# A selective scan whose initial values are folded into the first decay of each chunk

## The chip, the cores and the metric

The kernel runs on one core of one Trainium2 chip. The metric is device time in microseconds (us), from launch to end, as the median of several runs. A core has five engines with instruction streams of their own: PE (TensorE, matrix products), DVE (VectorE), ACT (ScalarE, activation functions), POOL (GpSimd) and SP (SyncE, which here issues transfers). [...] SBUF and PSUM are the two on-chip memories, both with 128 partitions.

## The reference

Two layers of a vision state-space model run one after the other on an image batch of 8 x 64 x 64 x 192. Each layer normalizes, projects to 384 channels, runs a 3x3 depthwise convolution, and scans the 4096 pixels of every image in several directions (layer 0: two, layer 1: four). Cut to the part that matters, the scan of one direction is:

```python
def step(h, inp):                                  # h: [b, K, 384, 16]
    u_t, dl_t, B_t, C_t = inp
    dA = jnp.exp(dl_t[..., None] * As[None])       # the decay
    h = dA * h + (dl_t * u_t)[..., None] * B_t[:, :, None, :]
    y = jnp.einsum('bkdn,bkn->bkd', h, C_t)
    return (h, y)
_, ys = lax.scan(step, h0, (u_l, dl_l, B_l, C_l))  # h0 = 0
```

`dl_t` is a softplus of a projection of the input. Each of 384 channels has 16 states, so there are 6144 independent first-order recurrences for each image and direction. Afterwards the directions are added, layer-normalized, gated and projected back.

## The kernel before, in words

**Tiling.** The 384 channels are three groups of 128 partitions (`DT = 3`). The 4096 pixels are cut into eight chunks of `T = 512`, the 16 states into eight pairs (`NP = 8`). One chunk of one direction of one image is a step `i`. It has 24 slots (`NSL`): a slot is one pair of states `m` and one channel group `dt`. There are 128 steps in layer 0 and 256 in layer 1; the eight steps of one direction of one image, a pass, follow one another, and `ci` counts them from 0. Half of the directions run backwards through the pixels (`rev`).

**What a slot does.** On PE, `inject` (L693) makes the inputs `hb` of the two recurrences in PSUM (two buffers). On ACT, `decay` (L713) makes the two rows of decays `da`, two Exps over 512 elements with the channel's `a_neg` as scale (five buffers). On DVE, `scan` (L728) runs two `tensor_tensor_scan` instructions: each computes o[t] = a[t] * o[t-1] + v[t] along 512 elements and needs a value to start from. In the first chunk of a pass that is the constant 0.0; in the other seven it is a column of the small tile `st`, which holds the states at the end of the chunk before. On POOL the result `h` is multiplied with the broadcast `C` rows (`cr`) into `hc`. On PE `reduce` (L752) sums `hc` over states into `py`. Every third slot `carry` (L747), on ACT, copies the last column of `h` (the first in a backward pass) into `st`. `h` has two buffers and `hc` and `cr` three, each for three slots.

**What else is in a step.** While step i is scanned, the inputs of step i+1 are prepared: `dt_proj` and `dt_bias` (the projection, L613 and L625), `dt_softplus` (L637, a softplus over `delta` with an ACT table load in front of it and one behind it that brings back the exponential set), `turn_delta` and `make_dut` (L655, L663). Finishing work of the image before (functions `f_...`: normalization, gate, output projection) is spread over the steps: in layer 0 in a rhythm of two steps, in layer 1 of four. Most of PE's small results go through one PSUM bank, tag "m", which holds one tile at a time.

**What sets the order.** Nothing is scheduled automatically here. `at(i, s, f, ...)` notes that function f is issued at slot s of step i; slot numbers stand in the tables `L0_SLOTS` and `L1_SLOTS`. At each slot the loop at L1049 issues the scan, then what is noted for the slot, then `inject` for two slots ahead and `decay` for four slots ahead. Each engine takes its instructions in this order, and waits are added where data or buffers demand it.

Of the kernel before, what the change touches and what calls it, by code (L numbers as in the profile page):

```python
# [8 lines left out]
F32 = mybir.dt.float32  # L9
AF = mybir.ActivationFunctionType  # L10
# [5 lines left out]
P = 128  # L16
# [8 lines left out]
DT = 3  # L25
NS = 16
T = 512
# [6 lines left out]
NP = NS // 2  # L34
# [476 lines left out]
def scans(tc, name, x_src, x_dst, xcd, xcd_col, xtd, xdd, t, dirs, rank, row_b, gate, slots, last, consts, dram):  # L511
# [5 lines left out]
    nc = tc.nc  # L517
# [3 lines left out]
    dtb, a_neg, lnw, lnb = t["dtb"], t["a_neg"], t["lnw"], t["lnb"]  # L521
    K = len(dirs)
    R = row_b + 2 * NS
    NSL = NP * DT
# [13 lines left out]
    steps = []  # L538
# [6 lines left out]
    with tc.tile_pool(name=f"{name}_s1", bufs=1) as s1, tc.tile_pool(  # L545
        name=f"{name}_s2", bufs=2
    ) as s2, tc.tile_pool(name=f"{name}_psy", bufs=1, space=PSUM) as psy, tc.tile_pool(
        name=f"{name}_psh", bufs=2, space=PSUM
    ) as psh:
        st = s1.tile([P, DT, 2, NP], F32, name="st")  # L550
        todo = {}

        def at(i, s, f, *a):
            todo.setdefault(i * NSL + s, []).append((f, a))

        live = {}
# [80 lines left out]
        def dt_softplus(i):  # L637
            softplus(nc, live[i]["delta"], live[i]["delta"])

            nc.scalar.preload_act_table_set("natural_log_exp_and_others")  # L640

        def load_xt(i):

            b, k, cols, rev, ci, c = steps[i]
            live[i]["xt"] = s1.tile([P, GC, D], F32, name="xt_k")
            for r in range(2):
                if cols:
                    w = c * RB + r * GC
                    src = xtd[b].rearrange("(h w) d -> h w d", w=W)[:, w : w + GC]
                else:  # L650
                    l = c * T + r * GC * G
                    src = xtd[b][l : l + GC * G].rearrange("(g j) d -> j g d", j=G)
                nc.sync.dma_start(out=live[i]["xt"][r * G : (r + 1) * G], in_=src)
# [59 lines left out]
        def decay(g):  # L713

            i, s = divmod(g, NSL)
            m, dt = divmod(s, DT)
            k = steps[i][1]
            da = s2.tile([P, 2, T], F32, name="da", bufs=5)
            for n in range(2):
                nc.scalar.activation(  # L720
                    da[:, n].rearrange("p (r g j) -> p r g j", r=2, j=G),
                    live[i]["delta"][:, dt].rearrange("p (g r j) -> p r g j", r=2, j=G),
                    AF.Exp,
                    scale=a_neg[:, k, dt, 2 * m + n : 2 * m + n + 1],
                )
            live[i]["da", s] = da

        def scan(i, s):  # L728
            m, dt = divmod(s, DT)
            b, k, cols, rev, ci, c = steps[i]  # L730
            hb, da = live[i].pop(("hb", s)), live[i].pop(("da", s))
            if dt == 0:
                live[i]["h", m] = (
                    s2.tile([P, DT, 2, T], F32, name="h"),
                    s2.tile([P, DT, 2, T], F32, name="hc", bufs=3),
                )
            h, hc = live[i]["h", m]
            for n in range(2):
                o, a = h[:, dt, n], da[:, n]
                v = hb.rearrange("p r (j n) -> p n (r j)", n=2)[:, n]  # L740
                if rev:
                    o, a, v = o[:, ::-1], a[:, ::-1], v[:, ::-1]
                init = 0.0 if ci == 0 else st[:, dt, n, m : m + 1]
                nc.vector.tensor_tensor_scan(o, a, v, init, ALU.mult, ALU.add)  # L744
            nc.gpsimd.tensor_mul(hc[:, dt], h[:, dt], live[i]["cr", m])  # L745

# [193 lines left out]
        def thrice(i, s, f, *a):  # L940
            for p, q in enumerate(s):
                at(i, q, f, *a, p)

        for i in range(N):
            j = i - 1
            live[i] = {}
            at(j, -3, load_xt, i)
            if xdd is None:
                at(j, -8, load_x, i)
                thrice(j, slots["x_proj"], x_proj, i)  # L950
                at(j, slots["x_dbl"], x_dbl, i)
            else:
                at(j, -4, load_xdbl, i)
            at(j, slots["turn_b"], turn_b, i)
            at(j, slots["keep_b"], keep_b, i)
            for dt in range(DT):
                for f in dt_proj, dt_bias, turn_delta, make_dut:
                    at(j, slots[f.__name__][dt], f, i, dt)
            at(j, slots["softplus"], dt_softplus, i)
            at(i, -12, load_b, i, 0)  # L960
            at(i, 0, load_b, i, 1)
            for m in range(NP):
                at(i, 3 * m - 6, load_c, i, m)
                at(i, 3 * m + 3, carry, i, m)
                for n in range(2):
                    at(i, 3 * m + slots["reduce"][n], reduce, i, m, n)
            b, k, cols, rev, ci, c = steps[i]
            if k and dirs[k - 1][0] != cols:
                for j in range(4 * DT):
                    at(i, 8 + j, load_turned, i, j)  # L970
                at(i, slots["add_turned"], add_y, i)
            else:
                at(i, 6, load_y, i)
                at(i, slots["add_y"], add_y, i)
            at(i, slots["keep_y"], keep_y, i)
# [24 lines left out]
        for c in range(NCH):  # L1000
            b, e, own = B - 1, N - NCH + c + 1, last
# [45 lines left out]
        with tc.manual_schedule(engines=ENGINES):  # L1047
            g = min(todo)
            while todo:  # L1049
                i, s = divmod(g, NSL)  # L1050
                if 0 <= g < N * NSL:
                    scan(i, s)
                for f, a in sorted(todo.pop(g, []), key=lambda fa: rank_of.get(fa[0], 1.5)):
                    f(*a)
                if 0 <= g + 2 < N * NSL:
                    inject(g + 2)
                if 0 <= g + 4 < N * NSL:
                    decay(g + 4)
                g += 1


def vss_layer(tc, name, x_src, x_dst, w, dirs, rank, row_b, gate, slots, last, consts, dram):

    with ExitStack() as ctx:
        xcd, xcd_col, xtd, xdd, *dram = dram
        if any(cols for cols, rev in dirs):
            xdd = None
        else:
            xcd_col = None
        t = load_weights(tc, ctx, name, w, len(dirs), rank, row_b + 2 * NS, consts[1])  # L1070
        clear = dram[-1] if xcd_col is None else ()
        front(tc, name, x_src, xcd, xcd_col, xtd, xdd, w["in_proj"][:, :D], t, clear, consts)
        scans(tc, name, x_src, x_dst, xcd, xcd_col, xtd, xdd, t, dirs, rank, row_b, gate, slots, last, consts, dram)
# [99 lines left out]
```

## Time and profile before

| What | us |
|---|---|
| Median of three runs | 25840.9 (25839.86 to 25843.88) |
| The profiled execution's own time | 25837.38 |
| Its span, first to last instruction | 25835.2 |
| of it before the scans of layer 0 (normalization, projection, convolution) | 954.8 |
| scans of layer 0, 128 steps | 8064.2, 63.0 each |
| before the scans of layer 1 | 1128.9 |
| scans of layer 1, 256 steps | 15650.8, 61.1 each |
| the end after the last scan | 36.5 |

The stretches are read from the starts and ends of scan instructions in the timeline. In layer 0's scan stretch DVE is busy for 7737.5 us and PE for 7553.0; in layer 1's DVE for 15184.5 us, PE for 14786.6, POOL for 14642.7 and ACT for 10885.3. The mean granted clock of TensorE was 0.991. DMA moved 160 GB/s on average.

In the groups of the page a line gives the source line, the engine, the operation, the tiles written and read with their shapes, and how often it ran; then the busy time in us with the mean duration of one in ns; then the idle time of its engine just ahead of it and who ended most of that. Where instructions of one engine overlap, the busy time counts a moment once, so it can be less than the count times the mean.

### The profile page before, as it was taken

The page shows a single profiled execution, that of the slowest core. Times are in us where ns is not written, and L with a number is a line of the kernel's source. Part 1 is how long each engine was busy: PE and PEld are TensorE (multiplying, and loading weights), DVE is VectorE, ACT ScalarE, POOL GpSimd, SP SyncE. Part 2 cuts the span into 40 slices and gives each one's busy share as a digit, 9 for nine tenths or more (in the row PEclk, how much of TensorE's full clock was granted, in tenths as well). Part 3 has the DMA queues.
Part 4 walks back from the last instruction along what each step waited for, and adds up shares of the span by engine and source line. Part 5 has one row for each costly group of instructions (what it writes and reads, how often), then busy time and mean ns, then how long its engine had stood idle before and what let it go on. Part 6 is the DMA issues. An engine that isn't in the chain of part 4 may idle for free.

```text
span 25835.2 us, 786127 instructions
## 1 busy us (share of the span) xinstructions
PE 24166.5 (94%) x340032; PEld 13568.7 (53%) x340032; DVE 24275.9 (94%) x22142; ACT 17771.4 (69%) x28068; POOL 22094.0 (86%) x9615
## 2 busy tenths in 40 slices
PE   9999999999999988999999999999999999999999
PEld 4555555555555534555555555555555555555554
DVE  7899999999999856999999999999999999999998
ACT  5667777777777656667666766766767767766766
POOL 0499999999999702999999999999999999999997
PEclk9999999999999999999999999999999999999999
DMA  4566666666666545575575575575575575575574
GB/s 164 153 154 156 154 156 158 155 155 156 154 157 156 133 161 173 164 160 165 166 161 167 166 160 166 166 161 167 166 161 167 166 159 167 165 161 167 164 163 141
DMA packets 3836347, 4140.60 MB, mean 160 GB/s; under 512 B 2140460, under 2 KB 2340804, under 8 KB 3829828
## 3 DMA queue, kind: packets, MB, share of 16 engines
q1 hardware_dynamic: 3821296, 4032.72, 60.5%
q8 instruction: 2692, 44.11, 0.7%
q10 hardware_dynamic: 11604, 57.59, 0.6%
q14 instruction: 755, 6.18, 0.1%
HBM read 3443.63 MB, written 645.99 MB: 158 GB/s over the span
## 4 chain that ended last, share of the span: by engine, by line
DVE 25%; PE 24%; issue 6%; ACT 6%; DMA 0%; POOL 0%; DVEq 0%; SPq 0%; ACTq 0%; POOLq 0%
DVE h L744 23%; PE hb L703 11%; PE py L151 7%; PE pd L568 2%; PE pt L616 2%; ACT da L720 2%; DVE dut L666 1%; PE pz L843 1%; ACT delta L144 1%; PE po L922 1%; ACT L144 1%; ACT L640 1%; ACT delta L630 1%; PE pq L658 0%; ACT xn_sq L831 0%
## 5 line engine op out<-in xcount | busy, mean ns | idle before, releaser
L745 POOL TENSOR_TENSOR hc<-h,cr 128x1024 f32<-128x1024 f32 x9216 | 21629.2, 2368 | 3610.2 <-DMA xt_k<-xtd 2022.4
L744 DVE TENSOR_TENSOR_SCAN h<-da,st,hb 128x512 f32<-128x512 f32 x16128 | 19191.2, 1259 | 625.2 <-PE hb L703 541.2
L720 ACT ACTIVATE da<-delta,a_neg 128x512 f32<-128x512 f32 x18432 | 12142.9, 713 | 3210.4 <-DVE h L744 3204.1
L703 PEld LDWEIGHTS hb<-dg,dut 64*128 64x128 f32 x147456 | 9256.7, 185 | 7063.8 <-issue 5863.5
L703 PE MATMUL hb<-dg,dut 64*128 64x128 f32 x147456 | 10905.4, 286 | 896.3 <-DVE h L744 622.7
L151 PE MATMUL py<-hc,mask 32*32 32x512 f32 x147456 | 6871.1, 602 | 0.2
L151 PEld LDWEIGHTS py<-hc,mask 32*32 32x32 f32 x147456 | 1568.4, 103 | 2341.7 <-issue 1746.8
L744 DVE TENSOR_TENSOR_SCAN h<-da,hb 128x512 f32<-128x512 f32 x2304 | 2611.3, 1200 | 121.7 <-PE hb L703 113.7
L750 ACT COPY st<-h 128x6 f32<-128x6 f32 x2688 | 533.0, 198 | 1843.4 <-DVE h L744 1842.3
L616 PE MATMUL pt<-xdbl,w_dt 96*128 96x512 f32 (+1 forms) x2304 | 1301.1, 646 | 53.3 <-DVE yc L886 33.4
L355 DVE SCALAR_TENSOR_TENSOR tp<-pad,cw,tp 128x512 f32<-128x512 f32 x1344 | 988.3, 750 | 214.6 <-ACT tp L349 180.5
L658 PE MATMUL pq<-ident,delta 128*128 128x128 f32 x4608 | 760.4, 288 | 388.7 <-DVE dut L666 334.6
L630 ACT ACTIVATE delta<-pt,dtb 128x512 f32<-128x512 f32 x1152 | 783.8, 680 | 477.4 <-PE pt L616 477.0
L843 PE MATMUL pz<-xn_sq,w_in 96*128 96x512 f32 x1536 | 832.0, 641 | 36.3 <-ACT xn_sq L831 15.8
L666 DVE TENSOR_TENSOR dut<-pq,xt_k 128x512 f32<-128x512 f32 x1152 | 767.1, 666 | 81.0 <-PE pq L658 81.0
L568 PE MATMUL pd<-x_k,w_x 128*128 128x512 f32 x1536 | 798.1, 629 | 38.8 <-DVE yc L886 15.2
L922 PE MATMUL po<-yc,w_out 128*96 128x512 f32 x1536 | 782.8, 620 | 15.4 <-POOL yc L916 12.4
L658 PEld LDWEIGHTS pq<-ident,delta 128*128 128x128 f32 x4608 | 485.1, 141 | 588.0 <-DVE dut L666 473.4
L151 PE MATMUL pc<-pad,taps 32*32 32x512 f32 x13824 | 578.0, 593 | 19.1 <-ACT xo L370 17.0
L916 POOL TENSOR_TENSOR yc<-yc,g 128x512 f32<-128x512 f32 x384 | 490.1, 1279 | 109.3 <-ACT yc L907 106.4
L144 ACT ACTIVATE delta<-delta 128x1536 f32<-128x1536 f32 x384 | 570.5, 1486 | 4.3
L322 PE MATMUL pi<-x,w_x 128*128 128x512 f32 x768 | 407.2, 650 | 165.9 <-ACT x L302 116.5
(103 smaller groups left out, 9927.5 us busy)
## 6 DMA issues: line engine op xcount, KB each, us to landing
cr<-cscr SPq DMA_DIRECT2D x2048, 512.0 KB
dg<-dgd SPq DMA_DIRECT2D x1536, 512.0 KB
cr<-xdd SPq DMA_DIRECT2D x1024, 512.0 KB
xt_k<-xtd SPq DMA_DIRECT2D x768, 384.0 KB
xcd<-xo SPq DMA_DIRECT2D x128, 768.0 KB
xtd<-xv SPq DMA_DIRECT2D x128, 768.0 KB
y<-yrow SPq DMA_DIRECT2D x128, 768.0 KB
yc<-yrow SPq DMA_DIRECT2D x128, 768.0 KB
```

The source lines that it names most:

```text
L144: nc.scalar.activation(out, in_, AF.Softplus)
L151: nc.tensor.matmul(out[j * Q : (j + 1) * Q, dt], w[i * Q : (i + 1) * Q], x[i * Q : (i + 1) * Q], start=first, stop=last, tile_position=(i ...
L568: nc.tensor.matmul(live[i]["pd"][:R], w_x[:, dt, k, :], live[i]["x"][:, dt], start=(dt == 0), stop=(dt == DT - 1),)
L616: nc.tensor.matmul(pt, w_dt[:, k, dt * P : (dt + 1) * P], live[i]["xdbl"][:rank], start=True, stop=True,)
L630: nc.scalar.activation(live[i]["delta"][:, dt].rearrange("p (g r j) -> p r g j", r=2, j=G), live[i]["pt"].rearrange("p (r g j) -> p r g j" ...
L658: nc.tensor.transpose(pq[:, g], live[i]["delta"][:, dt, g * P : (g + 1) * P], ident)
L703: nc.tensor.matmul(hv[:, r, q], live[i]["dut"][r * G : (r + 1) * G, dt, q], dg[r * G : (r + 1) * G, q, :, 2 * mm : 2 * mm + 2], start=True ...
L720: nc.scalar.activation(da[:, n].rearrange("p (r g j) -> p r g j", r=2, j=G), live[i]["delta"][:, dt].rearrange("p (g r j) -> p r g j", r=2 ...
L744: nc.vector.tensor_tensor_scan(o, a, v, init, ALU.mult, ALU.add)
L745: nc.gpsimd.tensor_mul(hc[:, dt], h[:, dt], live[i]["cr", m])
L843: nc.tensor.matmul(fin["pz"], w_in[:, u, dt * P : (dt + 1) * P], fin["xn"][:, u], start=(u == 0), stop=(u == CT - 1),)
L922: nc.tensor.matmul(fin["po"][:CP], w_out[:, dt, u * CP : (u + 1) * CP], fin["y"][:, dt], start=(dt == 0), stop=(dt == DT - 1),)
```

## The change

All scans start from a constant, 1.0 in the chunks that used to start from `st`. What they started from is multiplied into the first decay beforehand: a[0] * s + v[0] is the same as (a[0] * s) * 1.0 + v[0]. "First" is the first column in a forward pass and the last in a backward one (`edge`).

Three pieces make that product. `first_decays`, one slot after the softplus of the coming step, computes the decays of that one column for all 16 states on ACT, into a small tile `a0` of 128 x 3 x 16. `enter`, on POOL, multiplies `a0` by `st`, in two halves: states of the first four pairs at slot 14 of the step before, the other four at slot 1 of the step itself (`NSL + 1` counted from the step before). Last, `decay` copies two elements of `a0` over the edge column of each `da` tile, on ACT behind its two Exps. None of this is issued for the first chunk of a pass. `carry` stays as it was.

```diff
+        def edge(rev):
+            return T - 1 if rev else 0
+
+        def first_decays(i):
+            b, k, cols, rev, ci, c = steps[i]
+            if ci == 0:
+                return
+            live[i]["a0"] = s2.tile([P, DT, NS], F32, name="a0")
+            for dt in range(DT):
+                nc.scalar.activation(
+                    live[i]["a0"][:, dt],
+                    a_neg[:, k, dt],
+                    AF.Exp,
+                    scale=live[i]["delta"][:, dt, edge(rev) : edge(rev) + 1],
+                )
+
+        def enter(i, half):
+            if steps[i][4] == 0:
+                return
+            ms = slice(half * NP // 2, (half + 1) * NP // 2)
+            a0 = live[i]["a0"].rearrange("p t (m n) -> p t m n", n=2)[:, :, ms]
+            nc.gpsimd.tensor_mul(a0, a0, st.rearrange("p t n m -> p t m n")[:, :, ms])
...
@@ decay
                     scale=a_neg[:, k, dt, 2 * m + n : 2 * m + n + 1],
                 )
+            if steps[i][4] > 0:
+                f = edge(steps[i][3])
+                nc.scalar.copy(da[:, :, f], live[i]["a0"][:, dt, 2 * m : 2 * m + 2])
             live[i]["da", s] = da
@@ scan
-                init = 0.0 if ci == 0 else st[:, dt, n, m : m + 1]
+                init = 0.0 if ci == 0 else 1.0
                 nc.vector.tensor_tensor_scan(o, a, v, init, ALU.mult, ALU.add)
@@ the plan, for each step i with j = i - 1
             at(j, slots["softplus"], dt_softplus, i)
+            at(j, slots["softplus"] + 1, first_decays, i)
+            at(j, 14, enter, i, 0)
+            at(j, NSL + 1, enter, i, 1)
```

## The prediction

> **What bounds the kernel now.** I read the page's busy line first, then its costliest groups, then the waits, then busy times chunk by chunk. The busy line:
>
> ```profile
> PE 24166.5 (94%) x340032; PEld 13568.7 (53%) x340032; DVE 24275.9 (94%) x22142; ACT 17771.4 (69%) x28068; POOL 22094.0 (86%) x9615
> ```
>
> No engine is alone at the top; ACT (ScalarE) has most room. The groups concerned:
>
> ```profile
> L745 POOL TENSOR_TENSOR hc<-h,cr 128x1024 f32<-128x1024 f32 x9216 | 21629.2, 2368 | 3610.2 <-DMA xt_k<-xtd 2022.4
> L744 DVE TENSOR_TENSOR_SCAN h<-da,st,hb 128x512 f32<-128x512 f32 x16128 | 19191.2, 1259 | 625.2 <-PE hb L703 541.2
> L720 ACT ACTIVATE da<-delta,a_neg 128x512 f32<-128x512 f32 x18432 | 12142.9, 713 | 3210.4 <-DVE h L744 3204.1
> ...
> L744 DVE TENSOR_TENSOR_SCAN h<-da,hb 128x512 f32<-128x512 f32 x2304 | 2611.3, 1200 | 121.7 <-PE hb L703 113.7
> L750 ACT COPY st<-h 128x6 f32<-128x6 f32 x2688 | 533.0, 198 | 1843.4 <-DVE h L744 1842.3
> ```
>
> The reader is to see two kinds of scan: 16,128 that read their initial value from `st`, and 2,304 (first chunks of a direction) that start from a constant. The second kind is 59 ns shorter. Back to back the instructions overlap, so what counts is the pitch. Four of each in a row, from the timeline:
>
> ```profile
> 987.66 4.54 DVE L744 TENSOR_TENSOR_SCAN h<-da,hb 128x512 f32<-128x512 f32 x4
> ```
> ```profile
> 5023.72 4.79 DVE L744 TENSOR_TENSOR_SCAN h<-da,st,hb 128x512 f32<-128x512 f32 x4
> ```
>
> (4.79 - 4.54)/4 = 62 ns; the median over all start-to-start times is 1171 against 1111 ns, so 60 ns. The waits:
>
> ```profile
> ACT da L720 <- DVE h L744: 3204.1, 3349, 3.2
> DVE h L744 <- PE hb L703: 654.9, 1069, 6.3
> PE hb L703 <- DVE h L744: 622.7, 1142, 1.8
> DVE h L744 <- ACT da L720: 42.2, 52, 2.8
> ```
>
> ACT waits for DVE, seldom the reverse; DVE and PE wait for each other in equal amounts. Last, five consecutive chunks (48 scans each) of layer 1, the first with constant initial values; columns are the stretch, its length, and each engine's busy time:
>
> ```profile
> core 0: us, PE busy (x) PEld busy (x) DVE busy (x) ACT busy (x) POOL busy (x), PEclk, DMA share, GB/s
> 15955.20:16016.30 61.10, 59.81 (x848) 32.82 (x838) 58.58 (x56) 42.48 (x70) 59.70 (x28) 1.00 0.52 152
> 16016.30:16077.40 61.10, 58.83 (x832) 32.27 (x828) 58.80 (x53) 42.34 (x69) 56.37 (x25) 1.00 0.65 189
> 16077.40:16136.40 59.00, 55.51 (x840) 31.34 (x828) 58.41 (x53) 40.60 (x66) 56.37 (x25) 1.00 0.58 160
> 16136.40:16196.50 60.10, 55.87 (x828) 31.59 (x828) 59.97 (x53) 44.29 (x69) 56.20 (x25) 1.00 0.57 163
> 16196.50:16259.40 62.90, 60.23 (x850) 33.01 (x840) 61.39 (x55) 43.61 (x72) 60.36 (x29) 1.00 0.51 148
> ```
>
> Chunks 0 and 4 carry the same finishing work and differ in the scans. This is the change's effect already in the trace: DVE works 2.81 us less in chunk 0, and the chunk is 1.8 us shorter, not 2.8, because PE (98% busy) and POOL (98%) are then in the way. Chunks 2 and 3 are DVE's alone (99% and 99.8%).
>
> **What the Trainium skill says.** "Perfetto Trace Analysis", Optimizing Scalar/DVE Operations, gives a data-access overhead of about 60 ns for DVE on SBUF per instruction. It does not say that a per-partition initial value pays it a second time; the trace shows 60 ns for it. "ScalarE: Activation LUTs", What ACT_TABLE_LOAD costs: an ACTIVATE takes 186 ns + 0.833 ns per element, 93 ns more for a pointer operand, and back-to-back ones overlap by 93 ns. That makes 706 ns for the decays (713 here) and 188 for a two-element copy (the six-element one here: 198). "SBUF — State Buffer", Terms, has DVE and GpSimd exclude each other on a shared port pair. A scan takes one stream from PSUM, and hc products run beside scans all through the timeline, so I charge nothing.
>
> **Part 1, scans from 1.0.** 16,128 x 60 ns = 968 us less on DVE, 2.9 us in each of 336 chunks (seven in eight of 384). I take 1.0 to cost what 0.0 costs, both being constants in the instruction.
>
> **Part 2, a copy behind each pair of decays.** 336 x 24 = 8,064 copies on ACT. In the order of instructions each copy waits for the Exp just before it, so it cannot overlap it: 93 ns of overlap lost, a wait of about 32 ns (the gap between the two dependent Ln and Exp of `pm`, L893 and L894), and 188 ns less the 93 that the next instruction overlaps. Sum 0.22 us per slot, 5.3 us per chunk. The lower bound is 0.11 us, the step from an `st` copy to the next Exp (1004.54 to 1004.65); the upper is 0.35, nothing overlapping and a second such wait (93 + 32 + 198 + 32 ns). ACT then has 46 to 53 us of work in chunks of 58 to 63. Cover: `da` has five buffers, and setting the end of each pair of Exps against its scan gives a lead of 8 to 10 us, smallest after the softplus with its two table loads: on average 2.1 us (slot 14, layer 0 chunks with finishing work) and 2.0 us (slot 15, layer 1 chunks 3 and 7). Some four slots run without a wait before these, so the lead shrinks to about 1 us but stays. If it is gone, DVE waits, and evacuations queued behind the copies on ACT (`g`, `delta`, `xdbl`, all through the one "m" bank) hold PE.
>
> **Part 3, first decays.** 1,008 Exps of 128x16 on ACT: 292 ns each by the same page, 0.2 in a row, 0.6 us per chunk, right behind the softplus; bounds 0.4 and 0.9. The exponential set is loaded already, so no table load.
>
> **Part 4, `enter` on POOL.** 672 products of 24 elements. The rows of 1024 elements (2368 ns) and 512 (1279, L916) give 2.13 ns per element and 190 ns fixed: 0.24 us, so 0.5 us per chunk (bounds 0.4 and 1.1, the latter two 128x192 memsets at L505). It counts where POOL is level with DVE: 24 hc of 2.35 us are 56.3 us, above the 55.6 that DVE will need in chunk 2. Its waits: half 0 stands behind the product of slot 14, and the scan of slot 18 cannot start before that product (two `h` buffers), while ACT needs the result only after the scan of slot 19; half 1 stands behind the product of slot 1, which the scan of slot 6 needs, and ACT wants it after the scan of slot 7. So ACT never waits for it long. No DMA and no queue of SP moves.
>
> **The sum.** Per chunk I take the largest of the three engines after the change and 2% of unavoidable idle (as in chunk 0). Layer 1: chunk 1 (and 5): PE 58.8, so 60.0, gain 1.1; chunk 2 (6): POOL 56.4 + 0.5, so 57.8 to 58, gain 1.2; chunk 3 (7): DVE 60.0 - 2.9 = 57.1, POOL 56.7, so 57.9, gain 2.2; chunk 4: 1.8 as shown. Chunks 1 to 7: 10.8 us; 32 passes: 346 us. Layer 0 (two-chunk rhythm): chunk 0 takes 62.8 against 64.5 for its like (mean of images 1 to 7, first direction), so 1.7 for chunks 2, 4, 6; odd chunks have PE 57.9 and DVE 58.7 in 60.9, down to 59.5, gain 1.4. That is 3 x 1.7 + 4 x 1.4 = 10.7 us, 16 passes: 171 us. Together 517. Off this, 0.5 us in 112 chunks whose ACT lead nearly vanishes: 56. Net 460 us. The profiled execution took 25,837.4 us (span 25,835.2) and the median is 25,840.9, 3.5 apart, too little to matter; from the median this gives 25,380.
>
> **Rivals.**
> (a) The whole DVE gain comes: 968 us less, 24,870, or up to 25,200 with part of the idle kept. For: DVE is 97% busy in layer 1's stretch. Against: chunk 0 kept 1.8 of 2.8, and PE's and POOL's own sums leave 58 us per chunk.
> (b) ACT and the "m" bank give most back: at 0.35 us per slot the lead of 2 us is used up, evacuations come late and PE stalls about 1 us per chunk more. 25,520 to 25,790.
> (c) Slower: ACT becomes the bound. If a copy with its wait costs 0.75 us of ACT per slot, layer 1's chunk 3 needs 44.3 + 18.9 = 63.2 us instead of 60.1, layer 0's heavy chunks 47.4 + 18.9 = 66.3 instead of 64.5; over all chunks some 340 us more, 26,180. It decides from about 0.6 us per slot. Against: four times the step seen for `st` copies.
>
> **How the numbers follow.** Forecast 0.55 (25,200 to 25,520), (a) 0.15, (b) 0.15, no change 0.03, (c) 0.12. The range 25,000 to 25,790 leaves out (c), no change and the bottom of (a). Half a per mille is the spread of the runs; I count 0.2% (52 us) as the least that tells: faster 0.85, same 0.03, slower 0.12.
>
> **What would show it.** All 18,432 scans at 1200 ns; DVE busy near 23,310 us; copies of about 0.19 us on ACT, 0.22 from pair to pair; ACT near 19,500 us (8,064 x 188 ns and 1,008 x 0.2 us more). POOL and PE at 95% or more, with waits of DVE for PE `hb` and POOL up by some 400 us. Wrong if scans from 1.0 still take 1259, if DVE waits for `da` by hundreds of us, or if POOL waits for ACT at `enter`.

## The result, and the profile after

The kernel after takes 25385.95 us (median of 4 runs, 25370.74 to 25395.67) against 25841.32 before: a ratio of 0.9823, 95% interval 0.9806 to 0.984. The forecast was 25,380. That the sum met the time so closely is in part luck, as will be seen: two of its terms were too small by some 40 us each, one a gain and one a cost.

First the page after, in the lines that answer to those shown of before: the busy line, and of the costliest groups those that the change touches.

```profile
PE 24066.6 (95%) x340032; PEld 13537.7 (53%) x340032; DVE 23346.1 (92%) x22142; ACT 19452.5 (77%) x37140; POOL 22144.3 (87%) x10287
...
L772 DVE TENSOR_TENSOR_SCAN h<-da,hb 128x512 f32<-128x512 f32 x18432 | 20859.1, 1199 | 1227.8 <-PE hb L728 998.7
L745 ACT ACTIVATE da<-delta,a_neg 128x512 f32<-128x512 f32 x18432 | 12249.1, 713 | 1730.2 <-DVE h L772 1702.6
...
L753 ACT COPY da<-a 128x2 f32<-128x2 f32 x8064 | 1562.6, 194 | 294.3 <-ACT da L745 1.5
L778 ACT COPY st<-h 128x6 f32<-128x6 f32 x2688 | 537.1, 200 | 1128.0 <-DVE h L772 1126.6
```

All scans are one group now, at 1199 ns. DVE is busy 929.8 us less (24275.9 to 23346.1), but the span is only 441.7 us shorter (25835.2 to 25393.5), so DVE idles 488.1 us more. Fewer than half of the microseconds taken off the busiest engine arrived. The waits after tell who holds them:

```profile
POOL hc L773 <- DVE h L772: 1097.3, 1578, 6.1
DVE h L772 <- PE hb L728: 998.7, 1737, 6.2
...
PE hb L728 <- DVE h L772: 416.1, 820, 2.9
...
DVE h L772 <- ACT st L778: 86.1, 159, 1.7
PE pq L683 <- ACT g L882: 84.4, 56, 1.5
DVE h L772 <- ACT da L753: 72.5, 127, 1.6
```

Before, DVE waited 654.9 us for PE's `hb` and PE 622.7 for DVE. Now it is 998.7 against 416.1: DVE is the one that waits. That is 344 of the 488 us; waits that the view puts down to ACT make up the rest. Those names need care. No scan reads `st` any more, so the releaser named there is not the true one; what it is shows further down, and the same doubt holds for `da`.

The added instructions, from the groups kept apart by shape, two of ACT and one of POOL:

```profile
L652 ACT ACTIVATE a<-a_neg,delta 128x16 f32<-128x16 f32 x1008 | 235.4, 296 | 0.0
```
```profile
L665 POOL TENSOR_TENSOR a<-a,st 128x24 f32<-128x24 f32 x672 | 164.3, 244 | 0.0
```

Last, the same five chunks of layer 1 (image 3, first direction) as were shown before:

```profile
15702.20:15763.20 61.00, 59.84 (x848) 32.78 (x838) 58.47 (x55) 43.91 (x77) 60.38 (x29) 1.00 0.56 156
15763.20:15824.30 61.10, 58.35 (x832) 32.18 (x830) 56.06 (x53) 47.37 (x96) 56.31 (x27) 1.00 0.65 187
15824.30:15881.70 57.40, 55.58 (x850) 31.30 (x828) 55.70 (x53) 45.61 (x93) 56.47 (x27) 1.00 0.59 167
15881.70:15939.40 57.70, 55.57 (x828) 31.70 (x828) 57.10 (x53) 49.16 (x96) 55.94 (x27) 1.00 0.60 167
15939.40:16001.00 61.60, 60.17 (x854) 32.77 (x838) 58.64 (x55) 48.61 (x99) 60.59 (x30) 1.00 0.55 155
```

DVE (third busy time of a row) has lost 2.7 to 2.9 us in each chunk but the first. The chunk times answer very unevenly: 0 in chunk 1, 1.6 in chunk 2, 2.4 in chunk 3, 1.3 in chunk 4. Chunk 1 is where to look.

### The profile page after: what moved, and what is told of

Same layout as the page of the kernel before. It is cut to its first block, busy times and chain, and to the rows that moved or that the text cites. A ratio compares the mean times of both kernels' runs of the same rounds, so it can differ in the third digit from the quotient of the medians.

```text
span 25393.5 us, 794487 instructions
## 1 busy us (share of the span) xinstructions
PE 24066.6 (95%) x340032; PEld 13537.7 (53%) x340032; DVE 23346.1 (92%) x22142; ACT 19452.5 (77%) x37140; POOL 22144.3 (87%) x10287
## 4 chain that ended last, share of the span: by engine, by line
PE 30%; DVE 17%; ACT 10%; issue 3%; DMA 0%; POOL 0%; DVEq 0%; SPq 0%; ACTq 0%; POOLq 0%
DVE h L772 16%; PE hb L728 14%; PE py L151 9%; ACT da L745 5%; PE pd L568 2%; PE pt L616 2%; PE pz L871 1%; PE po L950 1%; ACT delta L144 1%; ACT L144 1%; ACT L640 1%; ACT da L753 1%; DVE dut L691 1%; PE pq L683 1%; ACT delta L630 0%
## 5 line engine op out<-in xcount | busy, mean ns | idle before, releaser
L772 DVE TENSOR_TENSOR_SCAN h<-da,hb 128x512 f32<-128x512 f32 x18432 | 20859.1, 1199 | 1227.8 <-PE hb L728 998.7
L728 PE MATMUL hb<-dg,dut 64*128 64x128 f32 x147456 | 10836.9, 286 | 602.9 <-DVE h L772 416.1
L151 PE MATMUL py<-hc,mask 32*32 32x512 f32 x147456 | 6871.8, 602 | 35.6 <-ACT y L821 35.1
L753 ACT COPY da<-a 128x2 f32<-128x2 f32 x8064 | 1562.6, 194 | 294.3 <-ACT da L745 1.5
L821 ACT COPY y<-py 128x1536 f32<-128x1536 f32 x384 | 552.1, 1438 | 37.1 <-PE py L151 19.5
```

Source lines behind the costliest of these rows:

```text
L151: nc.tensor.matmul(out[j * Q : (j + 1) * Q, dt], w[i * Q : (i + 1) * Q], x[i * Q : (i + 1) * Q], start=first, stop=last, tile_position=(i ...
L728: nc.tensor.matmul(hv[:, r, q], live[i]["dut"][r * G : (r + 1) * G, dt, q], dg[r * G : (r + 1) * G, q, :, 2 * mm : 2 * mm + 2], start=True ...
L753: nc.scalar.copy(da[:, :, f], live[i]["a0"][:, dt, 2 * m : 2 * m + 2])
```

## The experiments

All are compared with runs of the kernel before on the same chip, as ratios; differences between experiments are differences of ratios times 25,835 us. Each ratio is known to about 0.0015, so a difference of two is known to some 55 us. Times of chunks are sharper: in the first two directions of layer 1 most repeat from image to image within 0.1 us. Where times of chunks are given, they run from the first scan of a chunk to that of the next, as means over images 1 to 7.

**Half of the change, without its price.** The copies and the two functions that prepare them are not issued:

```diff
-            if steps[i][4] > 0:
-                f = edge(steps[i][3])
-                nc.scalar.copy(da[:, :, f], live[i]["a0"][:, dt, 2 * m : 2 * m + 2])
...
-            at(j, slots["softplus"] + 1, first_decays, i)
-            at(j, 14, enter, i, 0)
-            at(j, NSL + 1, enter, i, 1)
```

> The kernel after without first_decays, enter and the copies: all scans start from a constant, nothing is added (the carried states are left out of the result). Theory: of the 968 us that DVE saves, PE and POOL let through about 520 to 560, so 25,280 to 25,320 us, 60 to 100 us less than the kernel after; that difference is the price of the added work on ACT and POOL. Rival (the added work gives back what is missing of the 968): 24,870 to 25,000 us, with DVE's idle time as in the kernel before.

Measured: 25,281 us, ratio 0.9786 (0.9772 to 0.9801), as the theory had it. So 0.9823 - 0.9786 is the price of the added work, 96 us (about 40 to 150 by the two intervals); the rest of DVE's saving is lost without any of it. The rival falls.

**The price without the gain.**

```diff
-                init = 0.0 if ci == 0 else 1.0
+                init = 0.0 if ci == 0 else st[:, dt, n, m : m + 1]
```

> The kernel after with the scans starting from st again, all added work kept (the carried state is then counted twice in the result). Theory: under a slower DVE the added work is hidden, 25,840 to 25,900 us. Rival (the added work costs the same wherever it stands): 80 us and more over the kernel before, 25,920 us or more.

Measured: 25,903 us, ratio 1.0026 (1.0017 to 1.0036), 67 us over the kernel before. That lies between theory and rival: the added work is not hidden under a slower DVE. Whether a part of it is, the totals do not tell (67 against 96 us). The chunks of the first direction of layer 1 show where the price is paid:

| chunk | before | after | no added work | added work alone |
|---|---|---|---|---|
| 1 | 61.08 | 61.06 | 59.98 | 62.15 |
| 2 | 59.03 | 57.37 | 57.37 | 59.02 |
| 3 | 60.13 | 57.77 | 57.77 | 60.11 |
| 4 | 62.88 | 61.62 | 61.08 | 62.93 |
| 5 | 61.07 | 61.05 | 59.98 | 62.13 |

In chunks 2 and 3 the 24 copies cost nothing at all. In chunk 4 the added work costs 0.5 us with the faster scans and nothing with the slower ones. In chunks 1 and 5 it costs 1.1 us with either kind of scan, which is just what the faster scans bring there. Layer 0 pays too: its chunks 2, 4 and 6, which carry finishing work, are about 1 us longer than without the added work (48 chunks, 46 us); why was not followed. In layer 1 one wait does it. In the kernel after, chunk 1, PE and then DVE and ACT in order of time:

```profile
15796.39 1.19 PE L728 MATMUL hb<-dg,dut 64*128 64x128 f32 x16
15799.09 0.66 PE L683 MATMUL pq<-ident,delta 128*128 128x128 f32 x4 [1.51 <-ACT g L882]
15799.67 1.11 PE L151 MATMUL py<-y,skip 32*32 32x512 f32 x24
15800.72 1.19 PE L728 MATMUL hb<-dg,dut 64*128 64x128 f32 x16
```
```profile
15797.70 2.33 DVE L772 TENSOR_TENSOR_SCAN h<-da,hb 128x512 f32<-128x512 f32 x2 [0.89 <-PE hb L728]
...
15802.06 2.33 DVE L772 TENSOR_TENSOR_SCAN h<-da,hb 128x512 f32<-128x512 f32 x2 [1.44 <-ACT st L778]
```
```profile
15793.54 1.28 ACT L640 ACT_TABLE_LOAD   x1
15794.83 1.33 ACT L745 ACTIVATE da<-delta,a_neg 128x512 f32<-128x512 f32 x2
15796.20 0.20 ACT L753 COPY da<-a 128x2 f32<-128x2 f32 x1
15796.30 0.20 ACT L778 COPY st<-h 128x6 f32<-128x6 f32 x1
15796.40 0.70 ACT L652 ACTIVATE a<-a_neg,delta 128x16 f32<-128x16 f32 x3
15797.01 1.32 ACT L745 ACTIVATE da<-delta,a_neg 128x512 f32<-128x512 f32 x2
15798.36 0.19 ACT L753 COPY da<-a 128x2 f32<-128x2 f32 x1
15798.45 0.58 ACT L882 COPY g<-pz 128x512 f32<-128x512 f32 x1
...
15801.86 0.20 ACT L778 COPY st<-h 128x6 f32<-128x6 f32 x1
```

PE's transposes of delta need bank m, which holds `pz` until ACT has copied it to `g`. ACT has just come out of the softplus and its two table loads, and ahead of the copy of `g` now stand two copies and three first decays, about 1.1 us. PE waits 1.51 us, and behind the transposes stand the addition of `y` to `py` and the next `hb`; so DVE's scan starts 1.44 us late. The view names the `st` copy, but the scan starts 0.15 us after the end of `hb` (15801.91), as the scan before it started 0.12 us after the end of its own, and `st` was being written until that very moment. In the waits PE's line for `g` was, before:

```profile
PE pq L658 <- ACT g L854: 24.5, 56, 0.4
```

It is 84.4 us after, in 56 waits both times: 60 us more.

**Take POOL out of the way, then PE.** Two experiments each leave part of the work out.

```diff
# POOL
-            nc.gpsimd.tensor_mul(hc[:, dt], h[:, dt], live[i]["cr", m])
+            nc.gpsimd.tensor_mul(hc[:, dt, 0], h[:, dt, 0], live[i]["cr", m][:, 0])
...
-                block_diag(nc, live[i]["py"], mask, hc[:, dt, n], dt, first, last)
+                block_diag(nc, live[i]["py"], mask, hc[:, dt, 0], dt, first, last)
```

> The kernel after with half of POOL's products (hc of the second state of a pair is left out, the sum takes the first state twice; PE's work is unchanged). POOL falls from 56 to about 31 us per chunk. If PE is the engine that took DVE's place: 25,250 to 25,390 us, at most 130 us less than the kernel after. Rival (POOL holds the chunks, 2.35 us per slot against 2.22 of DVE): 300 us less or more, 25,090 us or under.

```diff
# PE, in reduce
-            first, last = m == 0 and n == 0, m == NP - 1 and n == 1
+            first, last = m == 0 and n == 0, m == NP - 1 and n == 0
+            if n:
+                return
```

> The kernel after with half of PE's sums over states left out (the second state of each pair is not summed), 8 to 9 us less PE work per chunk; POOL as after. If PE is the engine that took DVE's place, the chunks fall to POOL's and DVE's own sums, 58 to 59.5 us: 24,600 to 24,850 us. Rival (POOL holds the chunks): 25,200 us or more.

Their busy lines, POOL's first:

```profile
PE 24029.8 (95%) x340032; PEld 13526.3 (53%) x340032; DVE 23343.8 (92%) x22142; ACT 19444.1 (77%) x37140; POOL 12346.7 (49%) x10287
```
```profile
PE 21439.8 (86%) x266304; PEld 12878.5 (52%) x266304; DVE 23269.2 (94%) x22142; ACT 19444.3 (78%) x37140; POOL 22062.4 (89%) x10287
```

Measured: with POOL's work nearly halved 25,339 us, ratio 0.9809 (0.9793 to 0.9826), not told apart from the kernel after; chunk 2, which POOL was supposed to hold, 57.44 us instead of 57.37. With 2627 us less on PE 24,806 us, ratio 0.9604 (0.959 to 0.9618); chunk 2 falls to 56.34. The first chunk of the same direction shows the two side by side, POOL's experiment first (columns as in the prediction):

```profile
15643.20:15704.30 61.10, 59.94 (x849) 32.87 (x839) 58.57 (x56) 43.95 (x77) 34.69 (x29) 1.00 0.52 151
```
```profile
15294.70:15354.10 59.40, 52.40 (x658) 31.56 (x648) 58.57 (x56) 43.80 (x77) 59.29 (x29) 1.00 0.56 158
```

With POOL at 34.69 us of work instead of 60.38 the chunk keeps its 61.1 us; with less on PE it falls to 59.4 though POOL is full. PE is what holds DVE in most chunks now; POOL's 98 to 99% in some of them was following, not leading. In chunk 3 neither does: it takes 57.88 us with less on PE and 57.77 in the kernel after, where DVE is itself 99% busy.

**Does the whole gain come with PE and POOL out of the way?** The kernel before with PE's part left out, then both kernels with both parts left out.

> The kernel before with half of PE's sums over states left out (the second state of each pair is not summed). To be read against the kernel after with the same part left out, 24,806 us. Theory: with PE out of the way more of DVE's 968 us comes through, but POOL is next: 25,320 to 25,420 us, a saving of 510 to 610. Rival (PE had nothing to do with it): the saving stays 455, 25,260 us.

> The kernel after with the second state of each pair left out on PE (its sum) and on POOL (its product). With neither in DVE's way: DVE's own sums plus what the added work on ACT holds up, 24,400 to 24,650 us. Rival (POOL is not in the way and ACT's added work holds the rest): about 24,760 to 24,800, as with PE's part alone left out.

> The kernel before with the same left out on PE and on POOL. DVE's sums plus half a us of idle per chunk: 25,250 to 25,420 us. The saving, against e12_both_less: theory 700 to 930 us, near DVE's 968, because PE and POOL together held the rest back; rival: about 670, what it was with PE's part alone left out.

| left out | before | after | saving of ratio | us |
|---|---|---|---|---|
| nothing | 1 | 0.9823 (0.9806 to 0.984) | 0.0177 | 457 |
| half of PE's sums | 0.9866 (0.985 to 0.9883) | 0.9604 (0.959 to 0.9618) | 0.0262 | 677 |
| and half of POOL's products | 0.9858 (0.9845 to 0.9872) | 0.9595 (0.9582 to 0.9608) | 0.0263 | 679 |

In us these are 25,476 and 24,806, then 25,466 and 24,786. PE accounts for another 220 us of DVE's saving (150 to 290 by the intervals), more than was expected; POOL for none, so the theory of PE and POOL together falls, and the times are those of the last two rivals. About 250 of the 930 us stay lost even then. Some 160 of them are lost in chunks 1 and 5 of layer 1: with both parts left out these save 20 us over all 64 of them, though DVE has 2.8 us less to do in each. That is where PE waits for `g` in bank m, and it does so more than in the kernel after:

```profile
PE pq L683 <- ACT g L884: 154.8, 98, 2.2
```

That this wait is what takes the 160 us there was not tested, and the rest was not taken apart.

**A dose.** The copy is made twice:

```diff
                nc.scalar.copy(da[:, :, f], live[i]["a0"][:, dt, 2 * m : 2 * m + 2])
+                nc.scalar.copy(da[:, :, f], live[i]["a0"][:, dt, 2 * m : 2 * m + 2])
```

> The kernel after with every copy into the decays made twice, the second waiting for the first: 0.22 us more of ACT per slot, as much again as the change added. Theory: the price is near in proportion, another 90 to 150 us, 25,480 to 25,540 us. Rival (beyond the first 0.22 us the lead of ACT is gone and DVE waits for da by the slot): 25,700 us or more, near the kernel before.

Measured: 25,681 us, ratio 0.9945 (0.9931 to 0.996). The second copy costs 0.0122, 315 us (260 to 370 by the intervals), some three times the 96 us of all that the change added, though it is no dearer by itself:

```profile
L754 ACT COPY da<-a 128x2 f32<-128x2 f32 x8064 | 1563.2, 194 | 257.4
L753 ACT COPY da<-a 128x2 f32<-128x2 f32 x8064 | 1562.3, 194 | 293.8 <-ACT da L745 1.1 <-POOL hc L774 0.4
```

In the waits of this kernel PE waits for late evacuations (copies of ACT out of PSUM) that cost little before:

```profile
DVE h L773 <- PE hb L728: 1240.4, 1897, 6.3
...
PE py L151 <- ACT y L822: 112.6, 165, 1.8
PE pq L683 <- ACT g L883: 109.5, 56, 2.0
...
PE pt L616 <- ACT bt L605: 69.2, 98, 1.0
```

PE waited 35.1 us for `y` in the kernel after and hardly for `bt` (0.6 us). With `g` that is 171 us more of waiting. DVE still does not wait for `da` by the slot (140 us put down to it in all, 107 in the kernel after); it waits for PE, which waits for ACT. So neither side of the expectation holds: not in proportion, and not through the route that the rival named. The granted TensorE clock was lower too, 0.988 against 0.992; what part of the 315 us goes with that stays open.

**Move the gate.** Layer 1's first two gate products go behind the transposes of delta; the third begins one slot later:

```diff
-    "f_gate": ((11, 12), (17, 18), (20, 22)),
-    "f_keep": (13, 19, 24),
+    "f_gate": ((16, 17), (18, 19), (21, 22)),
+    "f_keep": (18, 20, 24),
```

> The kernel after with layer 1's first two gate products moved from slots 11 and 17 to 16 and 18 of their step (copies out of PSUM from 13 and 19 to 18 and 20), so that the turns of delta at slots 13 to 15 no longer stand behind a copy on a late ACT in bank m. Theory: chunks 1 and 5 of a pass in layer 1 fall from 61.06 to 60.0 us, as without the added work; 56 such chunks, 60 us, so 25,320 to 25,340 us. Rival (PE holds these chunks whatever the order, or the wait turns up at the next user of the bank): 25,370 us or more.

Measured: 25,372 us, ratio 0.9825 (0.981 to 0.9839): nothing gained that can be told, and the time of the rival. The wait of `pq` for `g` has gone from the list, and chunks 1 and 5 fell to 60.1 us in the first two directions (chunk 1 to 61.25 from 62.03 in the fourth, little changed in the third). So this wait is what held them, as the theory had it. But chunks 2 and 6 rose by 0.3 in all four (57.37 to 57.72), and what is left over, about 20 us by layer 1's chunks, is too small to be told.

**Make the copy cheaper.** Each copy is issued behind the first Exp of the next slot, so that the Exp it depends on is long done:

```diff
             for n in range(2):
+                if n:
+                    stamp(g - 1)
                 nc.scalar.activation(
...
+        def stamp(g):
...
+            nc.scalar.copy(live[i]["da", s][:, :, f], live[i]["a0"][:, dt, 2 * m : 2 * m + 2])
```

> The kernel after with each copy placed behind the first Exp of the next slot, so that it neither waits for the Exp just ahead nor breaks the overlap of Exps; the same work. Theory: 0.125 us of ACT less per slot (93 ns of overlap and 32 ns of waiting), 3 us per chunk, which is more than half of the copies' cost; some 40 to 60 us of the 105 that the added work costs come back, 25,320 to 25,350 us. Rival (a later copy reaches its scan later, and where ACT leads by 1 us DVE waits): 25,386 us or more.

Measured: 25,407 us, ratio 0.9841 (0.9826 to 0.9855). ACT's busy time fell by the overlap that was computed, 19452.5 to 18671.2 us, 97 ns per copy; the time did not. In chunk 3 of layer 1 (ACT, then DVE):

```profile
15898.66 0.72 ACT L747 ACTIVATE da<-delta,a_neg 128x512 f32<-128x512 f32 x1
...
15903.47 1.28 ACT L144 ACT_TABLE_LOAD   x1
...
15907.56 0.72 ACT L747 ACTIVATE da<-delta,a_neg 128x512 f32<-128x512 f32 x1
15908.19 0.18 ACT L764 COPY da<-a 128x2 f32<-128x2 f32 x1
```
```profile
15908.40 2.33 DVE L782 TENSOR_TENSOR_SCAN h<-da,hb 128x512 f32<-128x512 f32 x2 [0.83 <-ACT da L764]
```

The copy of slot 14 now stands behind the softplus that lies between two decays, and its scan waits for it. The rival is right, at this one place of a chunk. So the copy still owed was made before the long activations:

```diff
         def dt_softplus(i):
+            if owed:
+                stamp(owed.pop())
             softplus(nc, live[i]["delta"], live[i]["delta"])
...
         def f_act(rstd_next=False):
+            if owed:
+                stamp(owed.pop())
```

> As e3_copy_later (each copy behind the first Exp of the next slot), but a copy still owed is made before the softplus and before the gate's activation, so that it does not stand behind four to eight us of table loads and long activations. All the work of the kernel after is kept. Theory: the DVE waits for da of e3_copy_later (0.8 to 1.2 us in chunks 3 and 7 of layer 1, at slot 13 in layer 0) go, its gains in chunks 1, 4 and 5 stay: 25,300 to 25,340 us. Rival (the later copy costs what it saves wherever it stands): 25,380 us or more.

> e10_copy_flush together with the gate slots of e5_gate_later. Theory: chunks 1 and 5 of layer 1 come down to about 60 us, chunks 2 and 6 rise by 0.3: 25,290 to 25,330 us, 10 to 20 us under e10_copy_flush. Rival (with the copies out of the way ACT's evacuations are in time, and moving them only shifts waits): same as e10_copy_flush or above.

Measured: 25,357 us, ratio 0.9813 (0.98 to 0.9827), and with the gate moved too 25,346 us, ratio 0.9811 (0.9797 to 0.9824). Both lie above the range of their theory; the first is also below that of its rival. Chunks 3 and 7 came back from 58.71 to 58.10 and 57.77 (57.77 and 57.86 in the kernel after) and chunk 4 is at 61.07. By ratio the two are 26 and 31 us below the kernel after, but the intervals overlap: no version was shown to beat it, nor the second to beat the first.

## Why the prediction was right

**Durations.** All held: scans 1199 ns (1200 forecast), `enter` 244 (240). The estimates worked out from the Trainium skill's "ScalarE: Activation LUTs", What ACT_TABLE_LOAD costs, were 188 ns for a copy and 292 for a first decay; measured were 194 and 296. DVE was busy 23,346 us (23,310), ACT 19,452 (19,500). The wait of a copy for its Exp shows as 294.3 us of idle time, 36 ns each, and the lost overlap as the 97 ns that moving the copy gave back.

**That PE would stop the gain.** Shown: by 220 us more saving once PE has less to do. The first chunk of a pass, which had constant initial values already in the kernel before, was the right place to look: it did not change (61.07 and 61.06 us), and chunk 4, which carries the same finishing work, came to 61.08 without the added work. Rival (a), the whole gain, failed on this.

**That POOL would stop it too.** This part of the mechanism was wrong. The prediction had PE and POOL in the way of the first chunk and POOL as the floor of chunk 2, and expected waits of DVE for POOL. These went from 4.8 us to 0.8, and halving POOL's work changed neither chunk (61.07 and 57.44 us).

**Terms that were mis-sized.** The gain before ACT's price was put at 517 us and measured 551 (25,832 on that chip less 25,281; 514 to 589 by the interval). ACT's price was put at 56 us and measured 96. The intervals of the totals would allow both forecasts; the chunks do not. From the first scan of a layer to its last, in one profiled execution of each kernel, the gain without the added work was 170 us in layer 0 (171 forecast) and 380 in layer 1 (346), and the price 51 us in layer 0 (24) and 64 in layer 1 (32); over their whole spans these two executions are 104 us apart. (The table before the change ends layer 0's scans 9 us early and layer 1's 11 us late.)

The gain that is missing in the forecast is that of chunks 2 and 6 of layer 1, 1.7 us instead of 1.2: POOL's work was taken as a floor with 2% idle on top, and POOL was busy 98.4% of chunk 2 (56.47 of 57.40 us) without leading. The other gains of layer 1's first direction held (1.1 in chunk 1, 2.4 against 2.2 in chunk 3, 1.8 in chunk 4). The price was mis-sized and in part misplaced. The prediction charged 0.5 us in 112 chunks: layer 1's 3 and 7, which paid nothing, and layer 0's 2, 4 and 6, which paid about 1. Layer 1's chunks 1 and 5, where nothing was charged, paid 1.1 in the first direction, and chunk 4 paid 0.5. That the missing gain and the missing price nearly cancel is luck.

Three smaller slips stand in the working. By its own rule of 2% idle, chunk 3 comes to 58.2 us and not 57.9, and layer 0's odd chunks to 59.1 and not 59.5; over all chunks that is 22 us less and 28 more. And the three runs of the kernel before lay within 0.16 per mille, not half of one.

**The cover.** The lead of `da` was forecast to shrink to about 1 us. Counted from the end of the Exps as there, it went from 2.0 to 1.2 us at slot 15 of chunk 3 of layer 1, and in layer 0's fifth chunk from 2.1 to 1.4 at slot 14 and from 2.5 to 0.9 at slot 15, first directions; the copy takes 0.2 of what is left. DVE waits put down to `da` rose from 42.2 to 107 us (72.5 and 34.8). In 98 of the 107 us, though, the scan starts 0.10 to 0.13 us after the last matmul of its `hb`, as it does where the view names PE, so most of them are likely waits for PE. The loss that the experiments pin down is the other one that Part 2 named, evacuations late behind the copies and the single bank m.

**Rivals (b) and (c).** (b)'s mechanism, late evacuations and PE stalls, took what layer 1's chunks 1 and 5 paid, some 53 us; its size was wrong. What layer 0 paid stays open. (c) put the point where the change would turn into a loss at 0.6 us of ACT per slot. At 0.45 (two copies, each 0.194 and a wait) 0.0055 of the gain was left, 142 us, and the last 0.23 had cost 315. On that slope the rest would be gone at about 0.55, an estimate from these two steps; it was not run.

**`enter`.** ACT's idle time before a copy is put down to POOL in 0.8 us of the whole run, as the argument from the two `h` buffers had it.

## What to carry to other kernels

Before pricing a saving on the busiest engine, look in the trace for instructions that already have the new form, and read what the stretches holding them cost: here one chunk in eight had it, and with it the gain before the price of the added work was forecast at 517 us where 551 came. An engine that is busy 98% of a stretch need not hold it; taking work away from it tells, as it did for PE and against POOL. Cheap work put on an engine with room need not be paid everywhere: here the charge that was explained fell where that engine had just come out of a long operation and another waited behind it for a buffer that exists once. Look for that place before spreading a charge over all chunks.

## What the runs showed that was not expected

That a per-partition initial value makes a scan of 512 elements 60 ns slower from start to start than a constant (1171 against 1111 ns) was read before the change; that the constant 1.0 costs what 0.0 costs was assumed there, and all 18,432 scans show it (1199 ns against 1200).

In the four kernels with half of the sums left out, where PE was busy 85 to 86% of the span, the granted TensorE clock was 0.972 to 0.977; it was 0.988 to 0.993 in the profiled executions of the others. Why it fell, and whether it cost those kernels time, was not tested.

In this kernel the price of a small instruction on ACT rose steeply with how many there were: 96 us for the first 0.23 us per slot with all that prepares it, 315 for the second, on an engine that was busy 77 and then 81% of the time.
